# A two-layer graph network in fp32 on one core: late relus, two more pairs by seven products, and the adjacency loaded behind the first statistics

## The chip, the cores and the metric

One core of one Trainium2 chip runs the whole kernel. The metric is the device time in microseconds (us). Besides timed runs there is one profiled execution, from which every duration below is taken. The engines are named as in the profile: PE (TensorE, matmuls and transposes), DVE (VectorE), ACT (ScalarE), POOL (GpSimd) and SP (SyncE, which here only issues transfers). Each engine works through its own queue in order and waits for the others by semaphores. All data is fp32; a product of 128 x 128 by 128 x 512 takes two matmul instructions in the trace, 0.43 us apart.

## The reference

Two residual layers on x of 16 images, 1024 nodes and 256 features. What matters, shortened:

```
h = relu(layernorm(x))
c_adj = mean of h over features;  A_s = symmetrized 2*| |sigmoid(c_m - c_n) - 0.5| - 0.5 |
g = relu((h^T @ (adj * A_s)) * para)                 # queries
k, v = h @ kv_w
x = x + attention(q, k, v), 4 heads of 64
h = relu(layernorm(x))
A_hat = D^-1/2 (adj + I) D^-1/2                      # same for all images
z1 = (A_hat @ h) @ W1^T + b1                         # 512 wide
z2 = relu(batchnorm(z1)) @ W2^T + b2                 # statistics over all 16 images
out = x + batchnorm(z2)
```

The two batch norms need statistics over all images. So the kernel has three stages: everything up to z1 for every image, then z2 for every image, then the output.

## The kernel before

**Start.** SP issues x of image 0 in four pieces (`load_x(0, 2)`, L188), then at once the eight 512 KB blocks of the adjacency (L202) and kv_w (L205). POOL meanwhile issues six small column transfers (b1, g1 and so on, L81). DVE takes the layer norm's statistics of the first four blocks of x (`Norm.stats`, L250 and L252), POOL the power -0.5 (L257), and DVE the shift (L263, placed behind the statistics of the next two blocks); ACT then normalizes (L278). PE's first work is `turn_adj(0)` (L957), the transposes of adjacency block 0, then the transposes that spread the row sums (L312 and L323), and after some ACT and DVE work the first graph product `f_gps` (L398).

**One image.** In `graph(b + 1, between)` PE multiplies h by eight weighted adjacency blocks (L398), with steps of other work put between the blocks by hand: `between[c]` lists what is issued on the other engines before block c. Among them, for image b, is its second layer norm: statistics at 2 and 4, and the relus of blocks 0 to 3 and 4 to 7 at 6 and 7 (L278, writing `f_h_b`). Then come the queries (L415, L416), the values (L423, copied by L430) and the keys. For b of 2 and above the keys are made by seven products in place of eight (L463 to L487): products add up in one PSUM bank x, and after each ACT copies the bank's state out (L474, L478, L482, L487) before the next product is added. Then `linear1` (also seven products, L690) needs sums of parts of h (`f_hs`, L683 to L686), and `linear1_seven` makes z1 (L796) and stores it to DRAM (L831). Then `attention`.

**End of stage 1.** After the last attention two linear 1 are left. In the first of them, `third()` transposes W2 through a PSUM tile of pool `ps_s` (`turned`, L1027) and ACT copies it (L1176). For the very last image z1 is made in the plain form (`linear1_out`, L877), with its first batch norm invertible in two halves.

**Last passes.** z1 is read back (`fetch`, L163), normalized by ACT (`relu_on`, L152) and multiplied by W2. Image 0 goes in the plain form (L1221, `plain`, `plain_out` L1349 on DVE), then `SEVEN`, images 1 to 12, by seven products for a pair of tiles (`Pair`, L1283: m1 to m7, `keep` copies on ACT at L1294, `add` on DVE at L1297), then `rest`, the four tiles of images 13 and 14, in the plain form, then the two tiles of image 15, which stay in PSUM. A pair uses six slots of pool `io` (15 slots of 4 KB a partition) and, for block (1, 0), one of the four slots tagged `z`. PSUM in this stage is one pool of eight banks, which is closed before the last two tiles.

**Output.** After the second batch norm's statistics, z2 of each image is scaled (`finish`, L1498 on ACT or L1500 on DVE), transposed by PE (L1516), added to x1 (L1549, DVE) and sent out on ACT's queue (L1550). x1 of images 0 to 6 and 9 has been loaded ahead (`load_x1`, L1205), images 7 and 8 follow when the last tiles' `z` slots are free, and each further image when an output transfer frees its slots.

The stages are written under a manual schedule: the order in the source is the order on every engine, SP included.

## Time and profile before

| | us |
|---|---|
| median of 3 runs (lowest, highest) | 2447.41 (2447.23, 2450.25) |
| the profiled execution | 2446.91 |
| its span, first to last instruction | 2445.0 |
| PE busy | 2390.1 (98%) |
| DVE busy | 1777.3 (73%) |
| ACT busy | 1316.7 (54%) |
| POOL busy | 308.2 (13%) |
| granted TensorE clock, mean | 0.996 |
| first graph product begins | 17.48 |
| last passes begin (first z2 product) | 2169.44 |
| first output transfer is issued | 2382.70 |

Moved over the span: 169.35 MB read from DRAM and 71.10 MB written. A row of the time line gives the start, the length, the engine, the line, the operation with output and inputs, their shape and the count; a bracket at its end gives the idle time of that engine before it and what ended it. A row of stretches gives, for each engine, the busy time with the number of instructions, and then the clock, the share of time in which the 16 DMA engines were busy, and GB/s. In the chain of waits the columns are the start, the length and what the time was spent on. Under "who waited for it" stand the total time and the number of waits. For each transfer the trace also holds the times at which its 16 parts landed.

### The profile page before, as it was taken

What the parts mean: (1) busy time and instruction counts of PE and PEld (TensorE: products, weight loads), DVE (VectorE), ACT (ScalarE), POOL (GpSimd) and SP (SyncE); (2) the same over time, 40 slices, a digit from 0 to 9 for tenths busy, and PEclk for the clock granted to TensorE, in tenths of its full rate; (3) what the DMA queues carried; (4) which work ended last, traced back from release to release, by engine and by line L of the source; (5) the groups of instructions that cost most, each with busy time, mean ns of one, the idle gap of its engine ahead of it and who ended that gap; (6) DMA issues with size and microseconds to landing.
All of it is one profiled execution on the core that took longest, in us unless ns stands there. A gap on an engine that the chain in (4) does not pass through costs nothing.

```text
span 2445.0 us, 24677 instructions
## 1 busy us (share of the span) xinstructions
PE 2390.1 (98%) x8050; PEld 1052.2 (43%) x8050; DVE 1777.3 (73%) x2440; ACT 1316.7 (54%) x1918; POOL 308.2 (13%) x546
## 2 busy tenths in 40 slices
PE   8999999999999999999999999999999999999995
PEld 4443444434343434344443434343444434434444
DVE  6878677685959596776859595958777687747746
ACT  6845556454636464654546364645546465346633
POOL 2030202020110303020202002030202020000000
PEclk9999999999999999999999999999999999999998
DMA  5041414232322424141422233241414211455569
GB/s 185 9 139 61 151 61 142 69 109 68 109 86 75 128 64 148 61 151 61 125 78 90 79 100 103 67 144 61 151 61 138 74 49 51 142 194 172 167 214 377
DMA packets 176632, 275.76 MB, mean 113 GB/s; under 512 B 37872, under 2 KB 121328, under 8 KB 176496
## 3 DMA queue, kind: packets, MB, share of 16 engines
q1 hardware_dynamic: 156336, 241.55, 30.6%
q0 software_dynamic: 15552, 15.77, 2.5%
q10 hardware_dynamic: 4608, 16.78, 1.7%
q8 instruction: 66, 1.08, 0.2%
q14 instruction: 70, 0.57, 0.1%
HBM read 169.35 MB, written 71.10 MB: 98 GB/s over the span
## 4 chain that ended last, share of the span: by engine, by line
PE 79%; DVE 11%; SPq 3%; DMA 3%; ACT 2%; issue 2%; POOL 1%; DVEq 0%; ACTq 0%; POOLq 0%
PE f_aps L690 15%; PE f_s L501 14%; PE f_o L542 14%; PE f_gps L398 13%; PE f_zps L796 5%; DVE f_acc L518 3%; PE f_vps L423 3%; PE f_zx L1283 3%; SPq L606 3%; PE f_zm L1283 2%; PE f_kpsx L464 2%; PE f_z2ps L1221 2%; PE f_kps L464 1%; ACT f_h_b L278 1%; DVE f_w L349 1%
## 5 line engine op out<-in xcount | busy, mean ns | idle before, releaser
L509 ACT ACTIVATE f_p<-f_s 128x1024 f32<-128x1024 f32 x512 | 477.3, 1048 | 153.4 <-PE f_s L501 153.3
L518 DVE TENSOR_TENSOR f_acc<-f_acc,f_p 128x1024 f32<-128x1024 f32 x384 | 470.4, 1225 | 41.1 <-ACT f_p L509 0.5
L501 PE MATMUL f_s<-f_qT,f_kT 64*128 64x512 f32 x2048 | 456.8, 596 | 0.0
L542 PE MATMUL f_o<-f_p,f_v 128*64 128x512 f32 x2048 | 453.6, 595 | 0.0
L398 PE MATMUL f_gps<-f_w,f_h_a 128*128 128x512 f32 x1024 | 444.7, 594 | 0.3 <-DVE f_w L336 0.3
L368 POOL DMA_DIRECT2D f_hT<-f_hQ x480 | 235.8, 499 | 1219.9 <-PE f_gps L398 1170.7
L501 PEld LDWEIGHTS f_s<-f_qT,f_kT 64*128 64x128 f32 x2048 | 190.7, 185 | 263.6 <-ACT f_p L509 117.3
L398 PEld LDWEIGHTS f_gps<-f_w,f_h_a 128*128 128x128 f32 x1024 | 192.8, 190 | 247.0 <-issue 229.8
L542 PEld LDWEIGHTS f_o<-f_p,f_v 128*64 128x64 f32 x2048 | 141.4, 137 | 304.3 <-issue 253.9
L349 DVE SCALAR_TENSOR_TENSOR f_w<-f_w,f_adj 128x1024 f32<-128x1024 f32 x127 | 153.8, 1212 | 38.8 <-ACT f_w L348 38.8
L345 ACT ACTIVATE f_w<-f_row,f_col 128x1024 f32<-128x1024 f32 x127 | 147.0, 1158 | 28.1 <-DMA f_row<-frow 18.7
L278 ACT ACTIVATE f_h_b<-f_x,f_shift_b,f_rstd_b 128x256 f32<-128x256 f32 x128 | 64.7, 587 | 161.0 <-DVE f_shift_b L263 161.0
L348 ACT ACTIVATE f_w<-f_w 128x1024 f32<-128x1024 f32 x127 | 134.3, 1058 | 4.0
L690 PE MATMUL f_aps<-f_ahatT,f_hs 128*128 128x512 f32 x256 | 115.1, 592 | 0.0
L690 PE MATMUL f_aps<-f_t,f_hs 128*128 128x512 f32 x256 | 112.5, 592 | 1.3 <-DVE f_hs L684 1.3
L423 PE MATMUL f_vps<-f_kvw,f_hT 128*128 128x256 f32 x512 | 113.1, 379 | 0.0
L690 PE MATMUL f_aps<-f_ahatT,f_h_b 128*128 128x512 f32 x256 | 112.6, 592 | 0.0
L278 ACT ACTIVATE f_h_a<-f_x,f_shift_a,f_rstd_a 128x256 f32<-128x256 f32 x126 | 73.8, 587 | 63.4 <-DVE f_shift_a L263 63.4
L423 PEld LDWEIGHTS f_vps<-f_kvw,f_hT 128*128 128x128 f32 x512 | 97.3, 190 | 20.1 <-issue 7.4
L515 DVE TENSOR_TENSOR f_acc<-f_p,f_p 128x1024 f32<-128x1024 f32 x64 | 76.2, 1191 | 15.3 <-ACT f_p L509 15.3
L584 ACT COPY f_recs<-f_rec 32x32 f32<-32x32 f32 x128 | 31.5, 246 | 98.6 <-DVE f_rec L576 97.5
L569 ACT COPY f_parts<-f_red 32x64 f32<-32x64 f32 x128 | 39.1, 305 | 78.4 <-DVE f_red L534 77.3
(230 smaller groups left out, 2694.8 us busy)
## 6 DMA issues: line engine op xcount, KB each, us to landing
f_t<-ft SPq DMA_DIRECT2D x84, 512.0 KB, 6.9
fz<-f_z SPq DMA_DIRECT2D x64, 512.0 KB, 9.7
f_x<-in_x_dram SPq DMA_DIRECT2D x31, 1024.0 KB, 7.8
f_zb<-fz SPq DMA_DIRECT2D x36, 512.0 KB, 4.2
f_para<-in_L_gnn_para_dram SPq DMA_DIRECT2D x32, 512.0 KB, 4.4
f_att<-f_oT SPq DMA_DIRECT2D x512, 32.0 KB, 1.9
fx<-f_x SPq DMA_DIRECT2D x16, 1024.0 KB, 6.5
f_x1t<-fx SPq DMA_DIRECT2D x32, 512.0 KB, 6.6
```

What stands on the lines that cost most here:

```text
L278: nc.scalar.activation(self.h[:, c, :], self.xt[:, c, :], AF.Relu, bias=self.shift[:, c : c + 1], scale=self.rstd[:, c : c + 1], accum_out ...
L345: nc.scalar.activation(w, rows[b], AF.Abs, bias=cols[b][:, c : c + 1], scale=0.5 / C)
L348: nc.scalar.activation(w, w, AF.Tanh)
L349: nc.vector.scalar_tensor_tensor(w, w, 1.0, adj_t[c], ALU.subtract, ALU.mult)
L368: queue.dma_start(to[ts(k, 32), ts(a, 32 * NC)], t[ts(a, 32), k].rearrange("i c r -> i (c r)"),)
L398: nc.tensor.matmul(gps[d][:, ts(g, 512)], hs[b][:, c, ts(d, P)], w[:, ts(g, 512)], start=(c == 0), stop=(c == NC - 1),)
L423: nc.tensor.matmul(ps[:, i, :], hT[e][:, ts(c4 + i, P)], kvw_t[:, e, C : 2 * C], start=(e == 0), stop=(e == CC - 1),)
L501: nc.tensor.matmul(ps[:, e, :], kT[rows_e, pair, ts(m, P)], qT[rows_e, pair, ts(g, 512)], start=True, stop=True,)
L509: nc.scalar.activation(p, ps, AF.Exp)
L518: nc.vector.tensor_add(acc_of[s], acc_of[s], p)
L542: nc.tensor.matmul(o_of[s][e * HD : (e + 1) * HD, :], v[:, m, ts(2 * pair + e, HD)], p[:, e, :], start=(m == 0), stop=(m == NC - 1),)
L690: nc.tensor.matmul(ps, left[:, m, :], right(m), start=not more and m == 0, stop=(m == KH - 1), skip_group_check=more,)
```

## The change

It has these parts:

1. The adjacency's blocks and kv_w are issued by `load_adj()`, after the statistics of the first four blocks of x. To tie them together, these statistics are written to a tile in the slot of block 6 (tag `w2n`), so that block 6 is issued first and has to wait for their last reader; the other blocks follow in SP's order.
2. Of the second layer norm's relus, blocks 4 to 7 move out of `between[7]` to the list `"late"`: for b of 2 and above two run after the first key copy and two after the second, else before the keys.
3. The sums of h for the very last linear 1 are made in the one before it, by `ending()`, ahead of four statistics.
4. W2's transposes go through two PSUM tiles of the pools `ps_o` and `ps_t` in place of one of `ps_s`.
5. `SEVEN` goes to image 14, and `rest` is gone. What was loaded behind image 12 (tiles 30 and 31, x1 of images 0 to 6) is loaded in the turns of images 13 and 14. In the turn of image 14 ACT's relus of tiles 30 and 31 stand before `keep(0, 1)` and `keep(1, 1)`.
6. PSUM in the last passes is two pools of four banks: `ps_x` for the bank x and the last tiles, `ps_z` for the rest. Image 0's tiles take their banks in the order 1, 0. The pool `io` is opened before `big`, so its addresses change.
7. The first pair's loads are issued before image 0's products, block (1, 0) last, and `plain_out` copies on ACT.
8. In the output, c = 0 of images 0 to 3 is scaled before the second half's statistics are known, c = 1 of images 1 to 3 is scaled by ACT, and for image 0 this comes after the additions.

```diff
@@ start
-        adj_t = []
-        for c in range(NC):
...
+        adj_t = {}
         kvw_t = big.tile([P, CC, 2 * C], F32, tag="kvw", name="f_kvw")
-        nc.sync.dma_start(kvw_t, kv_w.rearrange("(c p) d -> p c d", p=P))
+        def load_adj():
+            for c in (LASTING.index("w2n"), *range(NC)):
+                if c in adj_t:
+                    continue
...
+                nc.sync.dma_start(t, adj[ts(c, P), :])
+                adj_t[c] = t
+            nc.sync.dma_start(kvw_t, kv_w.rearrange("(c p) d -> p c d", p=P))
...
+            own = norm.st
+            norm.st = lasting.tile([P, NC, 6], F32, tag="w2n", name="f_st_a0_first")
             norm.stats(0, HALF)
+            norm.st = own
+            load_adj()
             norm.invert(0, HALF)
@@ graph
+            late = between.get("late", ())
             if b < 2:
+                for step in late:
+                    step()
...
             nc.vector.tensor_add(c(0, 0), c(0, 0), m2)
+            late[0]()
             mult(x, sums[:, 1], t2, True)
             nc.scalar.copy(c(1, 0), x)
+            late[1]()
...
-                    7: [lambda: norm.relu(4, NC)],
+                    "late": [lambda: norm.relu(4, 6), lambda: norm.relu(6, NC)],
@@ linear 1
+        def sums_of_h(b, h1):
...
+            s1, s2, s3, s4 = made or sums_of_h(b, h1)
...
             store(0, 1)
+            ending()
             stats(1, 1)
             stats(0, 1)
...
-                        nc.scalar.copy(
-                            w2T.rearrange("p f c -> p (f c)"), turned(w2n, CC, FC, "w2")
-                        )
+                        for n, (pool, tag) in enumerate(((ps_o, "o"), (ps_t, "t"))):
+                            ps = pool.tile([P, 2, CC, P], F32, tag=tag, name=f"f_w2ps_{n}")
...
+                        lambda: made.extend(sums_of_h(b, norm.h)),
...
+                    linear1_all(b, norm.h, thirds, nothing, nothing, nothing, made=made)
@@ last passes
+        io = stage.enter_context(tc.tile_pool(name="fio", bufs=NH * (AHEAD - 3) + 1))
         big = stage.enter_context(tc.tile_pool(name="fbig2", bufs=1))
-        io = stage.enter_context(tc.tile_pool(name="fio", bufs=NH * (AHEAD - 3) + 1))
...
+            ps_x = stage.enter_context(tc.tile_pool(name="fps_x", bufs=4, space=PSUM))
             zps = ExitStack()
-            ps_z = zps.enter_context(tc.tile_pool(name="fps_z", bufs=8, space=PSUM))
+            ps_z = zps.enter_context(tc.tile_pool(name="fps_z", bufs=4, space=PSUM))
...
                     self.b[0, 0] = fetch(t0, 0, new("b11"))
-                    self.b[1, 0] = fetch(t0, 2)
                     self.b[0, 1] = fetch(t1, 0, new("b12"))
                     self.b[1, 1] = fetch(t1, 2, new("b22"))
+                    self.b[1, 0] = fetch(t0, 2)
...
-                    nc.vector.tensor_copy(place(t, c), ps[c])
+                    nc.scalar.copy(place(t, c), ps[c])
...
-            SEVEN = range(1, B - 3)
-            rest = range(2 * SEVEN[-1] + 2, TT - 2)
+            SEVEN = range(1, B - 1)
...
+            begun = {t: [bank(f"f_z2ps_{t}_{c}") for c in range(CC)] for t in (1, 0)}
+            first = pairs[SEVEN[0]]
+            first.load()
...
                     pairs[p + 2].load()
+                elif p + 1 in pairs:
+                    for t, f2 in ((TT - 2, 0), (TT - 2, 2), (TT - 1, 0)):
+                        zs[t, f2] = fetch(t, f2)
+                    load_x1(0)
+                else:
+                    zs[TT - 1, 2] = fetch(TT - 1, 2)
+                    for n in range(1, AHEAD - 3):
+                        load_x1(n)
...
+                else:
+                    relu_all(TT - 2)
                 now.m6()
                 now.keep(0, 1)
                 now.m7()
...
+                else:
+                    relu_all(TT - 1)
                 now.m5()
                 now.keep(1, 1)
@@ output
+            EARLY = 4
+
             def by_scalar(b, c):
-                return c == 0 or b % 2 == 1
+                return c == 0 or b % 2 == 1 or 0 < b < EARLY
...
-                    finish(0, 0)
-                    finish(1, 0)
+                    for n in range(EARLY):
+                        finish(n, 0)
...
+                if b > 0:
+                    finish_soon(True)
                 for h in range(NH):
                     nc.vector.tensor_add(xt[h], xt[h], outs[h])
                     nc.scalar.dma_start(out_v[:, 4 * h : 4 * h + 4, :], xt[h])
+                if b == 0:
+                    finish_soon(True)
+                finish_soon(False)
```

## The prediction

> **What bounds it now.** The shares come first: TensorE (PE) is busy 98% of the span at a clock of 0.996, so work on another engine counts only where PE stands still for it, or where PE has nothing left to do. I then looked for those places with the time line of PE, in order of time, reading the bracket that names the idle time and what ended it. They lie at the two ends.

> The start, in the chain of waits: PE's first work waits for the first adjacency block, and all that follows hangs on it without a gap.

> ```profile
> 2.78 7.35 DMA f_adj<-in_adj_dram
> 10.13 0.14 issue
> 10.27 1.94 PE f_adjps L957 x8
> 12.21 1.71 PE f_rps L312 x8
> 13.92 1.57 PE f_rps L323 x8
> ```

> The middle repeats every 133.3 us per image with PE closed up, but for one wait, which the question "who waited for L474" gives: the copy of the first key product comes late, and in 4 of 14 images PE itself stops.

> ```profile
>   PEld f_kpsx L464: 13.2, 14
>   DVE f_kT L476: 8.5, 4
>   PE f_kpsx L464: 2.9, 4
> ```

> The end of linear 1 and the last passes, PE's time line: seven stops in 240 us.

> ```profile
> 2123.34 1.98 PE L796 MATMUL f_zps<-f_zt,f_w1T 128*128 128x512 f32 x4 [1.39 <-ACT f_w2T L1176]
> ...
> 2136.90 7.11 PE L690 MATMUL f_aps<-f_t,f_hs 128*128 128x512 f32 x16 [1.28 <-DVE f_hs L684]
> ...
> 2169.44 14.00 PE L1221 MATMUL f_z2ps<-f_z,f_w2T 128*128 128x512 f32 x32 [1.40 <-ACT f_z L886]
> ...
> 2186.60 1.98 PE L1283 MATMUL f_zm<-f_z,f_w2T 128*128 128x512 f32 x4 [1.44 <-ACT f_z L152]
> 2189.77 1.96 PE L1283 MATMUL f_zx<-f_zt,f_w2s 128*128 128x512 f32 x4 [1.18 <-DVE f_zt L1278]
> ...
> 2200.57 1.98 PE L1283 MATMUL f_zm<-f_zt,f_w2T 128*128 128x512 f32 x4 [1.98 <-DVE f_z L1297]
> ...
> 2331.32 3.70 PE L1221 MATMUL f_z2ps<-f_zz,f_w2T 128*128 128x512 f32 x8 [1.39 <-ACT f_zz L152]
> ...
> 2363.31 10.54 PE L1221 MATMUL f_z2ps<-f_z,f_w2T 128*128 128x512 f32 x24 [0.83 <-issue]
> ```

> The output, by stretches (the last two numbers are the DMA share and GB/s): from 2390 us on all DMA engines are full, and the end is the end of the transfers. PE work saved before 2380 us still moves the end, because DMA is only 46% busy from 2340 to 2375 us.

> ```profile
> 2375.00:2380.00 5.00, 3.45 (x19) 2.55 (x17) 2.10 (x10) 0.88 (x1) 0.55 (x1) 1.00 0.60 198
> 2380.00:2385.00 5.00, 3.28 (x24) 2.57 (x24) 4.21 (x6) 3.86 (x4) 0.00 (x0) 1.00 0.65 254
> ...
> 2395.00:2400.00 5.00, 3.64 (x28) 2.74 (x26) 4.83 (x5) 1.98 (x2) 0.00 (x0) 1.00 1.03 415
> ```

> A stop is counted below from start to start of the matmuls less their usual pitch (0.43 us for one of 512 columns), so it is about 0.15 us more than the bracket.

> **Adjacency behind the first statistics: +0.9 us.** SP's nine issues (eight blocks, kv_w) now wait for the fourth bn_aggr, which ends at 5.32 us; before, the first was issued at 2.78. Behind them on SP stand the second image's x and W1, but x waits for the last relu at 12.1 us anyway. What could this buy? The third and fourth pieces of x land at 7.14 and 8.28 us, and DVE and ACT wait for them. [...] In the trace six of the 16 parts of the third piece land by 5.17 us, the other ten each right after a part of b1's small GpSimd transfer; the first adjacency packet moves only at 5.4 us, and the blocks then land in order, 10.13, 11.46, 12.75 us, 1.3 apart. [...] so the adjacency, behind x in SP's queue, doesn't hold x up, and waiting frees nothing. [...] the slowest DMA engine is busy with x until nearly 8 us in both kernels, so the first block to go lands near 10.1 as before. But that is now block 6, and block 0, which PE needs, comes second: 11.4, a loss of 1.3. [...] were the adjacency what holds x, x would be whole at 6, the shift could run when GpSimd's power is done (7.3, now 8.2), and block 0 could land at 9.6: a gain of 0.7. At the worst both transfers start a latency late: a loss of 1.8. I take 0.9, nearer to the row. W1 is needed by PE at 25.4 and lands at 24.9; it shifts no more than PE does.

> **Late relus: −3.4 us.** Of the eight relus (8 in 4.04 us) four move behind the first two key copies. ACT then reaches the queries 2.0 us earlier, and the stops, 0.92, 1.07, 1.09 and 0.40 us in four images (3.48 together), all shorter than 2.0, go. The price is to be hidden between the copies of L474, L478 and L482, where ACT idles 1.22 us each time; two relus take 1.01 and a tail of 0.08. It fits by 0.1 us. Without that cover each overrun would stop PE, as the next product accumulates in the bank being copied. In the image seen the last relu would end near 295.8, and the sums of linear 1 want h at 297.7. Bounds: 3.5 gained, 0.5 lost (0.02 per copy). For b = 1 only transfers are passed: nothing.

> **W2's transposes and the sums of h: −1.9.** The stops are 1.55 (m4 waits for the bank of the transposes) and 1.44 (the second factor s2 waits behind four bn_stats, 2.46 us). Both causes go, 2.99 together. But next is DVE: m4 is released by L852 at 2127.8, behind relu work that hangs on the attention's last addition, not on PE. PE now wants the bank at 2127.0 and gets it 0.8 later; s2 is ready at 2134.3, just before its product at about 2135, which was at 2136.9. I take 1.9; bounds 1.4 and 2.9.

> **First products of the last passes: −1.3.** Stop 1.57, for a bank still read by ACT (L886). Two other banks, long free, are taken now; next is ACT's relu of the first half, which ends at 2168.1, 0.25 after PE is free. Bounds 0 and 1.6.

> **The first pair: −3.4.** Its three stops are 1.61, 1.34 and 2.14, 5.09 together. Its loads were issued at 2172.2 to 2174.0, each behind the z slot that PE freed at 2172.9; now three of four go out right after the last store (2169.7), and block (1,0) after the slot. They land some 2.4 us earlier, and the fourth near 2181.7, its relu ending at 2183.3. Then ACT, not the load, is late: four plain_out copies (0.5 each) have moved to it, standing behind that relu, and m2 needs the bank that the third frees: about 2185.0, where PE would be there at 2183.4. So 1.6 of the 5.1 is given back. DVE, free of the copies, no longer causes the stop at m4. Bounds 1.5 and 5.1.

> **Two more pairs by seven products: −3.4.** The plain tiles of images 13 and 14 are 64 matmuls in the trace (8 + 56 of L1221 on f_zz); a pair by seven products is 28, in 12.02 us. 64 − 56 = 8, by 0.429 us: 3.4, all on PE. The additions (six of 0.67 to 1.23 us a pair) lie beside PE as in the twelve pairs before.

> **The seams: −1.2.** The stops before the plain tiles (1.55) and before the last tiles (0.99) go. A new one comes in pair 14: no next product stands between m5 and m3, so m3 waits for keep(1, 1), and that stands on ACT behind the relu of tile 31, whose second half is loaded only after m2 frees its slot: about 1.3. Bounds 0.5 and 2.3.

> **Output: −0.7.** Two c = 0 blocks more are scaled by ACT in its idle 4.26 us before 2380.1 (2 × 1.19), and DVE loses one scaling of 0.81 (image 2) before the DMA engines are full. The transfers past that point are the same bytes. Bounds 0 and 1.2. Reordered pools move addresses; I see no wait that they add.

> **The sum:** +0.9 − 3.4 − 1.9 − 1.3 − 3.4 − 3.4 − 1.2 − 0.7 = −14.4. The profiled execution took 2446.9 (span 2445.0), so 2432.5; the median of the runs shown is 0.5 higher, 2447.4, so 2433.0.

> **Rivals.**
> *Given back at both ends* (0.17): block 0 lands late (+1.8, 0.9 more), the first pair gains only its 1.5 (1.9 less), the seams 0.5 (0.7 less), the output nothing (0.7 less): −10.2, 2437.2. For it: all are queues worked out only to within a microsecond. Against: each needs its bad end.
> *x is freed* (0.12): the start gains 0.7 and the first pair all its 5.1: −17.7, 2429.7. For it: the wait for x's last pieces is real (DVE stands 4.1 us for x); against: the parts that landed late follow b1, not the adjacency.
> *The transfers are late for the output* (0.06): x1 of images 1 to 6, 6.3 MB, now starts in pair 14, with 3.1 MB more before the output. At 417 GB/s that is 22.6 us in some 33; if three images were still under way when the output starts, 7.5 us come back: 2440.5. Against: 10 us of slack.
> *Slower* (0.04): the relus behind the key copies don't fit. The two relus hold the accumulating product in each of 14 images twice; from an overrun of 0.51 us each (14.4 / 28) the change loses. If they ran with nothing overlapped, at the mean of 0.587 and a wait of about 0.6 before each pair, 1.8 us in a window of 1.22: 28 × 0.6 = 16.8 lost, 2449.8. Against: 8 in 4.04 us.
> The forecast keeps 0.61.

> **Numbers.** The terms' bounds, taken as independent, make about ±3; the range 2429.0 to 2438.5 takes in the second rival and most of the first. 0.2% (4.9 us) is what a measurement can tell from none. Faster 0.95, within it 0.02, slower 0.03.

> **What would show it.** Block 0's landing and the first f_gps (17.48 before): later means right. No idle before f_kpsx in any image. One short stop near 2127, none at the h sums. 14 pairs at 12.0 us. m2 of the first pair waiting for ACT. DMA full from about 2375 to the end. The forecast is wrong if f_gps starts earlier, if the key section takes over 6.4 us in all images, or if the DMA engines stop being full in the output.

## The result, and the profile after

| | before | after |
|---|---|---|
| median of the runs of both in one session (lowest, highest) | 2447.3 (2442.22, 2450.25) | 2435.02 (2433.29, 2436.68) |
| the profiled execution, its span | 2446.91, 2445.0 | 2434.83, 2432.8 |
| first f_gps begins | 17.48 | 18.99 |
| first z2 product begins | 2169.44 | 2165.46 |
| PE's first transposes of the output | 2377.93 | 2363.99 |
| first output transfer issued | 2382.70 | 2368.75 |
| from there to the last landing, to the end of the span | 60.2, 62.3 | 61.6, 64.1 |

The ratio is 0.9953 with a 95% interval of 0.9941 to 0.9966: some 12 us faster, where 14.4 less was forecast (2433.0, with 2435.02 inside the range). The table says where to look: the start lost 1.5, everything up to the output gained 15.5 beyond that, and the output gave back 1.8. The same places as before follow, in order of time.

The chain of waits at the start (start, length, what). Block 0 now lands at 11.93, and PE, ACT and the first product hang on it as before.

```profile
5.75 6.18 DMA f_adj<-in_adj_dram
11.93 0.14 issue
12.06 1.94 PE f_adjps L977 x8
14.00 1.72 PE f_rps L316 x8
...
15.74 0.69 ACT f_w L333
```

Who waited for the copy of the first key product (L481, which was L474): only the weight loads, 0.7 an image, and PE itself no longer stands among them.

```profile
who waited for it (us, times):
  PEld f_kpsx L471: 9.8, 14
```

PE's time line at the end of linear 1, in the last passes, and in pair 14. Of the eight stops shown of before one is left, 1.41 before the first z2 product, and two are new: 0.83 for the bank of m4 and 1.31 in pair 14. The first pair (2179.30 on) has none.

```profile
2126.05 7.11 PE L707 MATMUL f_aps<-f_ahatT,f_h_b 128*128 128x512 f32 x16 [0.83 <-DVE f_z L869]
...
2165.46 14.00 PE L1265 MATMUL f_z2ps<-f_z,f_w2T 128*128 128x512 f32 x32 [1.41 <-ACT f_z L904]
2179.30 1.88 PE L1327 MATMUL f_zx<-f_zb,f_w2T 128*128 128x512 f32 x4
2181.01 1.88 PE L1327 MATMUL f_zm<-f_z,f_w2T 128*128 128x512 f32 x4
...
2345.91 1.98 PE L1327 MATMUL f_zx<-f_zb,f_w2s 128*128 128x512 f32 x4 [1.31 <-ACT f_z L1338]
```

The output by stretches of 3.41 us (after the length: PE, PEld, DVE, ACT, POOL busy with counts, then the granted clock, the DMA share and GB/s). PE is busy 1.34 of 3.41 us in the second stretch, and in the third, where the output's transposes begin in earnest, its clock is 0.50.

```profile
2361.36:2364.78 3.42, 2.90 (x18) 2.36 (x16) 1.06 (x4) 2.85 (x3) 0.00 (x0) 1.00 0.92 352
2364.78:2368.19 3.41, 1.34 (x11) 0.86 (x9) 2.13 (x8) 1.95 (x2) 0.56 (x1) 1.00 0.76 279
2368.19:2371.60 3.41, 2.83 (x13) 2.83 (x14) 2.48 (x3) 1.33 (x2) 0.00 (x0) 0.50 0.61 243
```

PE's own rows show the two stops in those stretches, 1.77 and 0.88. They are the same in the kernel before (first two rows: before, last two: after); in the changed kernel the second stretch holds the first stop whole and 0.30 of the second.

```profile
2380.75 1.09 PE L1516 MATMUL f_outps<-f_ident,f_z 128*128 128x128 f32 x8 [1.77 <-DVE f_z L1500]
2382.72 2.23 PE L1516 MATMUL f_outps<-f_ident,f_z 128*128 128x128 f32 x16 [0.88 <-DVE f_x1t L1549]
...
2366.80 1.09 PE L1544 MATMUL f_outps<-f_ident,f_z 128*128 128x128 f32 x8 [1.77 <-DVE f_z L1526]
2368.77 4.38 PE L1544 MATMUL f_outps<-f_ident,f_z 128*128 128x128 f32 x24 [0.88 <-DVE f_x1t L1583]
```

That leaves four questions: why the start lost more than forecast, why the stop before the first z2 product stayed, why the first pair gained 5.1 and not 3.4, and what took 1.8 in the output. The runs below answer them, and test the late relus. Each was timed beside the kernel before; the differences from the changed kernel are mostly under 2 us, within the intervals of those ratios, so they are read in the profiles, by the stretch that the edit touches.

### The profile page after: what moved, and what is told of

Same layout as the page of the kernel before. It is cut to its first block, busy times and chain, and to the rows that moved or that the text cites. A ratio compares the mean times of both kernels' runs of the same rounds, so it can differ in the third digit from the quotient of the medians.

```text
span 2432.8 us, 24669 instructions
## 1 busy us (share of the span) xinstructions
PE 2386.7 (98%) x8042; PEld 1053.3 (43%) x8042; DVE 1782.0 (73%) x2441; ACT 1325.9 (55%) x1932; POOL 308.1 (13%) x546
## 4 chain that ended last, share of the span: by engine, by line
PE 96%; DMA 1%; DVE 1%; ACT 1%; issue 0%; POOL 0%; ACTq 0%; DVEq 0%; SPq 0%; POOLq 0%
PE f_s L510 19%; PE f_o L551 18%; PE f_gps L402 18%; PE f_aps L707 16%; PE f_zps L813 6%; PE f_vps L427 5%; PE f_zx L1327 4%; PE f_zm L1327 3%; PE f_kpsx L471 2%; PE f_kps L471 1%; PE f_z2ps L1265 1%; PE f_zps L895 1%; PE f_kps L444 1%; DMA out_dram<-f_x1t 1%; DVE f_x1t L1583 1%; PE f_zps3b L813 0%
```

## The experiments

### The start: what the wait costs

The first run issues the blocks in the order 0 to 7, at once behind x:

```diff
-            for c in (LASTING.index("w2n"), *range(NC)):
+            for c in range(NC):
...
+        load_adj()
...
-            norm.st = lasting.tile([P, NC, 6], F32, tag="w2n", name="f_st_a0_first")
             norm.stats(0, HALF)
-            norm.st = own
-            load_adj()
```

> The changed kernel (profiled span 2432.8), but SP issues the adjacency at once behind x, in the order 0 to 7, as before. Theory 1 (block 0 stands second and lands late: 11.93 against 10.13): the first f_gps goes back from 18.99 to about 17.5, the third and fourth pieces of x land again near 7.1 and 8.3, and the span falls by 1.5, to about 2431.3. Rival (the deferral buys something further on, since x is read sooner): the first f_gps comes no earlier than 18.6 and the span doesn't fall.

The second keeps the wait and lays the first statistics in the slot of block 0:

```diff
-    LASTING = ["z"] * 4 + [None] * 2 + ["w2n", "w2T"]
+    LASTING = ["w2n"] + ["z"] * 4 + [None] * 2 + ["w2T"]
```

> The changed kernel, but the tile of the first statistics lies in the slot of block 0 in place of block 6, so that block 0 is the first to go behind them. Theory 1 (the wait itself costs nothing; only block 0's second place does): block 0 lands about where block 6 did, near 9.6 to 10.7, x's last pieces stay at 6.3 and 7.15, PE transposes the row sums as soon as ACT and DVE have them (about 11.3, was 13.8), the first f_gps is at 16.5 to 17.2 (18.99), and the span falls by 1.8 to 2.5, to about 2430.7: below the kernel that issues at once (2431.3). Rival (waiting for the statistics costs by itself): the first f_gps is at 17.8 or later and the span stays above 2431.5.

e1: PE begins on block 0 at 10.10, f_gps begins at 17.39, the span is 2431.7 (time 2433.22, ratio 0.9951, 0.9934 to 0.9967). e2: f_gps at 15.79, 3.2 earlier than in the changed kernel, but the first z2 product at 2163.94, no earlier than in e1 (2163.86): 1.7 of the 3.2 is lost again, 1.3 of it in one stop 10 us later. Span 2431.0, time 2432.07 (0.9946, 0.993 to 0.9963). PE's time line of e2 shows where:

```profile
9.66 1.94 PE L977 MATMUL f_adjps<-f_ident,f_adj 128*128 128x128 f32 x8 [9.66 <-DMA f_adj<-in_adj_dram]
...
15.79 3.67 PE L402 MATMUL f_gps<-f_w,f_h_a 128*128 128x512 f32 x8 [0.26 <-DVE f_w L340]
...
25.88 1.06 PE L1047 MATMUL f_w1ps<-f_ident,f_w1n 128*128 128x128 f32 x8 [1.15 <-DMA f_w1n<-in_L_gnn_W_dram]
```

W1, behind 1 MB of x in SP's queue, lands at 25.75 and is the next bound. So the third run, otherwise like the second, moved it:

```diff
+            w1n = w4.tile([P, FC, C], F32, tag="w4", name="f_w1n")
+            nc.sync.dma_start(w1n, W1.rearrange("(f p) d -> p f d", p=P))
             xs[1] = load_x(1)
```

> Block 0 first behind the statistics, and W1 is issued ahead of the second image's x. With block 0 first alone the first f_gps was at 15.79, but PE then stopped 1.32 for W1, which lands at 25.75 behind 1 MB of x. Theory 1b (that transfer is what takes the gain back): W1 lands near 22.5, the stop goes, the stretch from the first f_gps to the first z2 product falls from 2148.1 to 2146.5 to 2146.9, and with f_gps at 15.8 the first z2 product is at 2162.3 to 2162.8 (2165.46 in the changed kernel). Rival (PE is held by what stands behind: the weighting of the blocks on ACT and DVE, or the second image's x landing late): the stretch stays at 2147.8 or more.

W1 lands at 22.06, its stop is gone, and the stretch from f_gps to the first z2 product is 2146.60, as in the changed kernel (2146.47). Here f_gps began at 16.98, so the first z2 product came at 2163.58 and not at the 2162.3 to 2162.8 expected; span 2431.4, time 2431.89 (0.9939, 0.9923 to 0.9956).

The scatter of this start has to be known before a single f_gps is believed. PE's first transposes of block 0 began at 10.27, 10.10 and 9.20 in three executions that issue at once (the third is e9, below), at 11.12 to 12.50, mean 11.9, in eight with block 0 second, and at 9.66, 9.73 and 10.51 in three with block 0 first. The first f_gps: 15.92 to 17.48, mean 16.9; 18.37 to 19.86, mean 19.0; 15.79 to 17.83, mean 16.9. So theory 1 is half right. Second place costs 2.1 us on average; for the wait as such no cost shows, within the scatter of three executions each. Nor does a gain: that e2 would go below issuing at once isn't borne out. x's last two pieces land at 6.2 to 6.7 and 7.0 to 7.4 in all eleven executions in which the adjacency waits. Where it doesn't, they land at 7.1 to 7.6 and 8.2 to 8.3 in two of three, and at 6.3 and 7.35 in the third (e9). So x was held up in two executions; the mean f_gps is the same either way.

### The first z2 product: the pool, not the bank

```diff
-            ps_z = zps.enter_context(tc.tile_pool(name="fps_z", bufs=4, space=PSUM))
+            ps_z = zps.enter_context(tc.tile_pool(name="fps_z", bufs=2, space=PSUM))
+            ps_y = zps.enter_context(tc.tile_pool(name="fps_y", bufs=2, space=PSUM))
-                return (pool or ps_z).tile([P, 512], F32, tag="z", name=name)
+                    pool = (ps_y, ps_y, ps_z, ps_z)[len(turns) % 4]
...
-            begun = {t: [bank(f"f_z2ps_{t}_{c}") for c in range(CC)] for t in (1, 0)}
+            begun = {t: [bank(f"f_z2ps_{t}_{c}") for c in range(CC)] for t in (0, 1)}
```

> The changed kernel, but the pool of four banks for the last passes is split in two pools of two, and tile 0 of image 0 takes the one that lies where ps_o and ps_t lay. Theory 2 (the first product waits because its bank belongs to a pool that lies over ps_s, and such a pool is handed over only when the last reader of ps_s is done, L904 at 2165.41, whatever the bank): the stop of 1.57 before the first f_z2ps shrinks to 0.2 or less, nothing new comes before 2200, and the span falls by 1.2 to 1.5, to about 2431.4. Rival (the wait is for the relu of the data, or the first pair's ACT queue takes the time back): the stop stays at 1.5 or the gain is found again as a stop between 2175 and 2190, and the span stays at 2432.8.

PE's time line of this run: the product starts behind the last one of linear 1, and nothing follows.

```profile
2159.75 4.03 PE L895 MATMUL f_zps<-f_aggT,f_w1T 128*128 128x512 f32 x9
2163.61 13.90 PE L1270 MATMUL f_z2ps<-f_z,f_w2T 128*128 128x512 f32 x32
2177.34 1.88 PE L1332 MATMUL f_zx<-f_zb,f_w2T 128*128 128x512 f32 x4
```

From f_gps to the first z2 product it is 2144.89, 1.58 less than 2146.47, and the first pair is as dense as in the changed kernel. Span 2429.1, time 2431.96 (0.9948, 0.9932 to 0.9965); the span lies 3.7 below that of the changed kernel, more than the stop, and the rest is in the output (below). In the changed kernel the bank of the first product (tile 0, c = 0) still lies over ps_s. ACT's rows of that kernel give the last two readers of ps_s:

```profile
2160.66 1.26 ACT L904 ACTIVATE f_z<-f_zps,f_b 128x512 f32<-128x512 f32 x2 [2.17 <-PE f_zps L895]
...
2164.14 1.27 ACT L904 ACTIVATE f_z<-f_zps,f_b 128x512 f32<-128x512 f32 x2
```

The bank's own last reader is the first of them, done at 2161.92, before PE was free. But PE waited for the other one, the last reader of all of ps_s, at 2165.41 (the bracket of 1.41 before 2165.46). In e3 the bank in a pool that lies only over ps_o and ps_t didn't wait (2163.61, without a bracket).

### The output: half the clock

Two runs: one has the scaling in the old order, the other fills PE's wait for the second half's statistics.

```diff
-            EARLY = 4
+            EARLY = 2
...
-                return c == 0 or b % 2 == 1 or 0 < b < EARLY
+                return c == 0 or b % 2 == 1
...
-                if b > 0:
-                    finish_soon(True)
+                finish_soon(True)
```

```diff
+                    for n in range(12):
+                        nc.tensor.transpose(outs[1][:, n % 4, ts(1, P)], ident, ident)
                     ready[0, 1] = z2[:, 1, 0, :]
```

> The changed kernel, but the output's scaling in the old order (two images ahead of the statistics, odd images' c = 1 on ACT, ACT's scaling ahead of the additions). From the first output transfer to the end of the span the kernel before takes 62.3, the changed one 64.05. Theory 3 (the new order of scaling costs it): back to about 62.3, span about 2431. Rival a (a half-speed window of the clock fell on the first transposes of the output, 2368.2 to 2371.6, and the transfers got into another order; chance of the windows): the time from first output to end depends on where such a window falls and not on the edit: 64 with one, 62.5 without one in the first 4 us. Rival b (x1 loads and addresses): stays at 64 without such a window.

> The changed kernel, with 12 transposes of the identity into the unused half of an output bank, later overwritten, in PE's 1.8 us wait for the second half's statistics (1.4 us of work, none of it on the path). In the runs so far a window of 3.41 us in which PE was busy 0.38 to 0.39 (2364 to 2368) was followed by one at half clock, and the time from the first output transfer to the end was then 63.1 to 64.6; after 0.48 or 0.51 it was not, and the end came after 62.3 to 62.5. Theory 5 (the half clock is the output's lost time): the windows before the output are busy 0.6 or more, the clock stays full until 2380, and first output to end is 62.2 to 62.8: span about 2431.2. Rival (the order of the scaling or of the transfers costs it): 63.7 or more with the clock at full speed.

e4: 63.1 from first output to end, with a half-clock window from 2370.6 (first output at 2371.11); span 2434.2, time 2434.05 (0.9953, 0.9937 to 0.997). A second window of that kind hit it at 2346.7, right behind the stop in pair 14, and its 3.41 us cost PE about 1.7. e7, in the same kind of stretches as above:

```profile
2363.08:2366.49 3.41, 2.88 (x18) 2.35 (x17) 1.05 (x4) 2.85 (x3) 0.00 (x0) 1.00 0.89 333
2366.49:2369.90 3.41, 2.66 (x23) 2.19 (x21) 2.13 (x8) 1.95 (x2) 0.56 (x1) 1.00 0.82 264
2369.90:2373.32 3.42, 2.60 (x20) 2.13 (x21) 3.37 (x4) 1.33 (x2) 0.00 (x0) 1.00 0.68 268
```

PE is busy 2.66 in place of 1.34 in the stretch of the wait, and the clock stays at 1.00. First output to end is 63.2, between the two expectations; span 2433.7, time 2433.45 (0.9946, 0.993 to 0.9963). What decides is the time from the first output transfer to the last landing, since 2.1 to 3.3 us more follow the last landing and vary without a pattern that I see:

| first output to last landing | us |
|---|---|
| before, twice (clock full) | 60.2, 59.9 |
| new order, clock full (e3, e5, e10) | 59.8, 59.6, 59.9 |
| new order, wait filled (e7, e11) | 59.9, 60.1 |
| new order, half clock (changed kernel, e1, e2, e6, e8, e12) | 61.6, 61.7, 61.1, 61.3, 61.3, 61.3 |
| old order, half clock (e4) | 61.0 |

With the clock full at the first transposes it is 60.2 at most, with half clock there 61.0 at least, whatever the order. (Later in the output every profile has half-clock windows: in before from 2404.52 and 2411.35, in the changed kernel from 2388.67, 2398.91 and 2405.74.) In the new order half clock costs 1.5. At full clock the new order gains 0.2 (its third output goes out 2.4 behind the first, not 3.0), which is hardly more than the scatter; at half clock the one profile of the old order is 0.4 below the mean of the new. So theory 3 has no room for 1.8, and neither has rival b. PE's stops are the same in both kernels, so where the window falls is chance: in the two profiles of before the window with the longer stop was busy 0.51 and 0.56, and half clock did not follow.

### The late relus

```diff
-                    "late": [lambda: norm.relu(4, 6), lambda: norm.relu(6, NC)],
+                    7: [lambda: norm.relu(4, NC)],
...
-            late[0]()
-            late[1]()
```

> The changed kernel, but blocks 4 to 7 of the second layer norm's relus go back to between[7]. Theory 4 (the prediction's: ACT reaches the queries 2.0 later, and that alone made PE stop ahead of the first key product of the next half): stops before f_kpsx return in about four of 14 images, 3.4 to 3.6 together, and the time from the first f_gps to the first z2 product grows from 2146.5 to about 2150.0. Rival (the stops went for another reason, such as the start's new phase): no stop of over 0.3 returns there and the stretch stays at 2146.5 to 2147.

One stop came back, 1.32 in one image, and the stretch grew by 1.47, to 2147.94 (span 2432.5, time 2434.86, ratio 0.9956, 0.9939 to 0.9972). Neither text had that. GpSimd's time line of this run shows the image that stopped, against the one before it:

```profile
949.99 1.66 POOL L261 TENSOR_TENSOR f_rstd_b<-f_var_b,f_mhalf 128x8 f32<-128x8 f32 x1 [3.49 <-DVE f_var_b L260]
...
1082.68 0.50 POOL L372 DMA_DIRECT2D f_hT<-f_hQ  x1 [0.22 <-issue]
1084.24 0.50 POOL L372 DMA_DIRECT2D f_hT<-f_hQ  x1 [1.06 <-DMA f_hT<-f_hQ]
1084.75 1.67 POOL L261 TENSOR_TENSOR f_rstd_b<-f_var_b,f_mhalf 128x8 f32<-128x8 f32 x1
```

In image 8 the power -0.5 stood behind two transfers that POOL issues, one of which waited for a landing: it began 1.8 after its input. DVE's shift and all of ACT's chain (relus, queries, values, the key copy) moved with it, and PE stopped:

```profile
1094.93 1.13 PE L471 MATMUL f_kpsx<-f_kt,f_kt 128*128 128x512 f32 x2 [1.16 <-ACT f_kT L481]
```

So the 2.0 us by which ACT is earlier are slack for delays that differ from execution to execution. A second profile of the kernel before (e9, below) shows how much they differ.

The late power is not the only such delay. In the first profile of before it accounts for one stop of four (the same image, 1.6 late); in the other three, and in both of e9, POOL was on time, but DVE's addition of the attention (L614) waited long for a transfer. DVE's rows of the kernel before, in an image with a stop and in one without:

```profile
946.73 1.23 DVE L614 TENSOR_TENSOR f_x<-f_x,f_att 128x1024 f32<-128x1024 f32 x1 [4.66 <-DMA f_att<-f_oT]
...
1213.25 1.23 DVE L614 TENSOR_TENSOR f_x<-f_x,f_att 128x1024 f32<-128x1024 f32 x1 [2.70 <-DMA f_att<-f_oT]
```

In the two profiles of before, the five images that stopped without a late power have the addition 22.9 to 23.8 behind the start of the graph product that it runs beside, those without a stop at 22.8 or less. In the changed kernel one image has it at 23.2, and PE doesn't stop: that is the slack at work. Why these transfers land late isn't shown.

### The first pair: chance or program, copies or order

Three edits, besides the second profile of before (e9). The loads stand behind image 0's products again (e8):

```diff
-            first.load()
             for t in range(2):
                 plain(t, begun[t], 0)
...
+            first.load()
             for k, j in ((0, 0), (0, 1), (1, 1), (1, 0)):
```

plain_out copies on DVE (e10):

```diff
-                    nc.scalar.copy(place(t, c), ps[c])
+                    nc.vector.tensor_copy(place(t, c), ps[c])
```

Block (1, 0) is loaded second (e12):

```diff
+                    self.b[1, 0] = fetch(t0, 2)
                     self.b[0, 1] = fetch(t1, 0, new("b12"))
                     self.b[1, 1] = fetch(t1, 2, new("b22"))
-                    self.b[1, 0] = fetch(t0, 2)
```

> The changed kernel, but the first pair's loads are issued behind image 0's products again (block (1, 0) still last, plain_out still on ACT). Theory 6 (the three stops of the first pair were waits for the loads, and going out 3 to 4 us earlier took all three): stops of 2.5 to 4 in all come back between the first f_zx and 2200, most of them before m2 and m4. Rival (the copies on ACT in place of DVE were what took them): less than 1.0 comes back.

> The kernel before, profiled a second time. Theory 7 (two of the terms are drawn anew in each execution: the stops ahead of the key products, since GpSimd's power -0.5 comes late in some images, and the first pair's loads, whose 4 KB packets took 0.2 to 0.47 on average and up to 1.6 in the first profile of before, 0.16 to 0.2 in that of after): the stops before f_kpsx sum to another amount than 3.48, and the three stops of the first pair to another amount than 5.09, each by over 0.7. Rival (both are fixed by the program): 3.3 to 3.7 in the same four images, and 4.8 to 5.4 in the first pair.

> The changed kernel, but plain_out copies on DVE again. Theory 8 (DVE's queue caused the last stop of the first pair, 2.14 before m4, and moving the copies to ACT removed it): a stop of 1.5 to 2.2 comes back before m4 (about 2191). Rival (that stop was late only because the loads were): DVE begins the first pair's sums about 2178 in place of 2186 after 8.3 more of the stretch, its copies then fit, and less than 0.5 comes back.

> The changed kernel, but block (1, 0) of each pair is loaded second again and not last. The copies on DVE alone brought back 1.48 before m2 and none of the other two stops (1.35 and 2.15 in the kernel before). Theory 9 (those two are the load order: blocks (0, 1) and (1, 1) stand behind (1, 0), which waits for its slot, and DVE's sums with them): the first sums begin 3 to 4.5 later than the 12.2 after the first z2 product seen now, and stops of 2.5 to 3.7 in all come back between the first f_zx and 2200. Rival (they come only if copies and order are both as before, since DVE then has both): less than 1.0 comes back.

e8: no stop at all in the first pair; its loads went out 2.6 us after the first z2 product, as in the changed kernel. SP gets to them no earlier, with or without the products behind them: after the last z1 store it stands 2.2 us for DVE's last aggregation of the first batch norm, which ends 2.5 behind the first z2 product. From SP's waits around it, the same line in the changed kernel and in e8:

```profile
SPq L163 <- DVE f_bn_mv L112: 2.2, 1, 2.2
```

Theory 6 falls (span 2433.8, time 2434.39, 0.995, 0.9933 to 0.9967). e9 splits: the key stops sum to 0.67 in two images (first profile: 3.48 in four), so they are drawn anew in each execution; the first pair's are 4.9, the same three, so they belong to the program. PE's time line of e9:

```profile
2182.96 1.98 PE L1283 MATMUL f_zm<-f_z,f_w2T 128*128 128x512 f32 x4 [1.25 <-ACT f_z L152]
2186.13 1.96 PE L1283 MATMUL f_zx<-f_zt,f_w2s 128*128 128x512 f32 x4 [1.19 <-DVE f_zt L1278]
...
2196.94 3.12 PE L1283 MATMUL f_zm<-f_zt,f_w2T 128*128 128x512 f32 x4 [1.99 <-DVE f_z L1297]
```

The last row takes 3.12 for four matmuls, where 1.98 is usual: the stops left a window busy only 0.42, and half clock followed, 1.7 lost on top (span 2442.8, time 2444.68 in its one run). e10 brings back one stop, 1.48, but before m2 and not m4, which neither of its texts had (span 2433.0, time 2435.17, one run):

```profile
2180.11 1.88 PE L1327 MATMUL f_zx<-f_zb,f_w2T 128*128 128x512 f32 x4
2183.31 1.95 PE L1327 MATMUL f_zm<-f_z,f_w2T 128*128 128x512 f32 x4 [1.32 <-ACT f_z L1338]
```

ACT's copy named there had ended at 2182.61; what ended last is DVE's first plain_out copy (2182.52 and 0.68), which frees the bank that m2 takes. e12 brings back 2.51, as theory 9 has it in sum, but all of it before m2, and with it a half-clock window that costs 1.7 more (span 2436.5, time 2438.37, one run):

```profile
2183.05 2.66 PE L1327 MATMUL f_zm<-f_z,f_w2T 128*128 128x512 f32 x4 [2.35 <-ACT f_z L1393]
2185.51 2.94 PE L1327 MATMUL f_zx<-f_zt,f_w2s 128*128 128x512 f32 x4
```

DVE's sums begin 16.2 after the first z2 product (changed kernel: 12.2; before: 16.4). So the order of the loads makes the sums and ACT's relus 4 us earlier, and the copies on ACT take DVE's part of the queue away; it took both to remove all the stops. Why the order matters so much is in the DMA's stretches. The kernel before, 5 to 9 us behind its first z2 product (last two numbers: DMA share, GB/s):

```profile
2174.44:2176.44 2.00, 2.00 (x6) 0.80 (x6) 0.52 (x2) 2.00 (x4) 0.00 (x0) 1.00 0.76 223
2176.44:2178.44 2.00, 2.00 (x6) 0.92 (x5) 0.00 (x0) 1.42 (x3) 0.00 (x0) 1.00 0.72 123
```

The changed kernel in the same place:

```profile
2170.46:2172.46 2.00, 2.00 (x6) 0.80 (x6) 0.52 (x2) 2.00 (x4) 0.00 (x0) 1.00 0.95 334
2172.46:2174.46 2.00, 2.00 (x6) 0.92 (x5) 0.00 (x0) 2.00 (x4) 0.00 (x0) 1.00 0.97 328
```

Blocks (0, 1) and (1, 1) landed 13.4 and 14.7 after the first z2 product in before, 7.9 and 10.6 in the changed kernel, while (1, 0), second or last, landed at 12.0 and 11.9. With (1, 0) second it was the same in e9 (252, then 160 GB/s) and in e12 (240, then 158). So it goes with the order. SP issues the other two 1.1 us later behind (1, 0)'s slot; why the transfers also run at half the rate isn't settled.

### All of it together

The kernel of e6 with e3's banks, e7's filled wait, and in pair 14 the last half tile's relu behind `keep(1, 1)`:

```diff
-                    relu_all(TT - 1)
+                    relu_on(zs[TT - 1, 0], 0)
                 now.m5()
                 now.keep(1, 1)
+                if not soon:
+                    relu_on(zs[TT - 1, 2], 2)
```

> The changed kernel with block 0 first, W1 ahead of x, own banks for the first product, the last half tile's relu behind keep(1, 1) (the 1.47 stop of pair 14), and the filled wait. By the separate measurements: the first f_gps at 16 to 17 in place of 18.99 (2.0 to 3.0), no stop before the first f_z2ps (1.6), none in pair 14 (1.5), no half clock at the output (1.4 less than the changed kernel's profile): span 2425.3 to 2426.5, and about 7 below the changed kernel in time, 2427 to 2429. If the gains hide behind one another (DMA in the output, or ACT's queue in the first pair), the span stays above 2428.

2429.22 (2428.65 to 2430.61, 5 runs), ratio to before 0.9935 (0.9922 to 0.9949), span 2428.6. The changed kernel's 2435.02 was timed beside other runs of before: by the ratios the gain over it is 0.0018, about 4.4 us, and the intervals overlap. The stop before the first z2 product and the half clock at the output are gone, but f_gps drew 17.83, and in pair 14 a stop of 0.84 stays:

```profile
2339.91 1.88 PE L1332 MATMUL f_zx<-f_zb,f_w2s 128*128 128x512 f32 x4
2342.47 1.98 PE L1332 MATMUL f_zx<-f_zb,f_w2s 128*128 128x512 f32 x4 [0.68 <-ACT f_z L1343]
```

m3 adds to the bank that keep(1, 1) copies, and with no other product in between the copy of 0.58 lies open. The expected 2425.3 to 2426.5 took the start at its best, this stop at nothing, and the end behind the last landing at 2.1 to 2.5 (here 3.2). The span lies above the 2428 that was set as the sign of gains hiding behind one another; these three misses, 0.8 to 1.8, 0.84 and 0.7 to 1.1, account for it without that.

## Why the prediction was right, point by point

The range was kept and most of the mechanisms were as told; three terms (first products, first pair, output) failed in whole or in part, and their errors partly cancelled. (The text counts seven stops in PE's 240 us where its own block shows eight; the terms use all eight.)

- **Adjacency, +0.9: too small.** The mechanism is as forecast: block 6 lands first, at 9.51, and block 0 comes second, at 11.93. The first block to land isn't later for the wait (before: 10.13). The term was sized by "11.4, a loss of 1.3"; in eight executions the loss at f_gps is 2.1, beyond the bound of 1.8 on average, 1.5 in the profiled pair. "Waiting frees nothing" failed: x's last pieces, at 6.2 to 6.7 and 7.0 to 7.4, came about 1 us sooner than in two of three executions at once (7.1 to 7.6 and 8.2 to 8.3). That the adjacency, behind x in SP's queue, doesn't hold x up was the author's estimate, and those two contradict it.
- **Late relus, −3.4: right between the two profiles (3.48), but not a property of the program.** "The stops, 3.48 together, all shorter than 2.0, go": they did, in every image of all eleven profiles with the late relus. Undone, they came back as 1.3, and a second profile of before had 0.67. The worth is 0.7 to 3.5 an execution. The forecast was sized on the profile with 3.48 and is compared here with that same profile, so the match says little of the size. The price was nothing, as forecast: two relus fit between the copies.
- **W2's transposes and sums, −1.9: measured −2.0.** Both stops went, and the one forecast to come ("gets it 0.8 later") is there at 2126.05, behind DVE's L869: 0.83 in the bracket, 0.99 by the prediction's count. Read in the profile alone; neither was undone by itself.
- **First products, −1.3: failed, 0.** The step "two other banks, long free, are taken now" was wrong: the bank's own history didn't count, since its pool lay over one still in use. With a pool of its own the gain was 1.58.
- **First pair, −3.4: measured −5.1, the mechanism half wrong.** The failed step is "the fourth near 2181.7": block (1, 0) landed at 2177.33, since its slot was free as soon as SP came to it. So ACT's copies, which were to give 1.6 back, weren't late. e12 shows the forecast wait exactly, m2 behind ACT's L1393, where that block's neighbours are late. The step "three of four go out right after the last store (2169.7)" was wrong too: they go out 2.6 behind the first z2 product in either place (e8). What made the sums early is the order among the loads, which the term did not count.
- **Two more pairs, −3.4.** Not tried alone; in the trace pairs begin every 12.02 us to the last, as forecast (once 0.34 more, for a small check product).
- **Seams, −1.2: measured −1.1.** 1.55 and 0.99 went, and the stop in pair 14 came, 1.47 where 1.3 was forecast, behind the relu named.
- **Output, −0.7: measured +1.8.** The term left out the clock. 1.5 of it is a half-clock window on the first transposes (2368.19 to 2371.60, clock 0.50), about 0.4 the end behind the last landing; the edit itself gained 0.2 at full clock. The DMA engines were full to the end, as forecast, but from 2380, not 2375 (share 0.92 from 2375 to 2380, 1.03 in the next 5 us, 1.02 from 2420 to 2425).

The terms as measured, 1.5 − 3.5 − 2.0 − 5.1 − 3.4 − 1.1 + 1.8, make −11.8 of the −12.2 between the profiles. So the forecast of −14.4 was right by its sum partly by luck: errors of +0.6, +1.3 and +2.5 stood against one of −1.7, and two of the terms, the key stops and the half clock, are drawn anew in each execution. The rival in which both ends give back (2437.2) had the loss at the start and the missing gain of the output right in place; the first pair and the seams did not give back as it said.

## What to carry to other kernels

Reordering loads behind a wait is judged by which transfer goes first, not by the wait (here second place cost block 0's consumer 2.1 us on average, and the wait showed no cost): look at the block that the first consumer needs. A new PSUM pool over an old one waited here for the old one's last reader (a stop of 1.41, and 1.58 gained without it), so the first tile of a new stage should lie in a pool over banks that nobody reads any more. And a stop of PE can cost more than its length: where stops left PE busy 0.38 to 0.42 of a window of 3.41 us here, half clock followed and took 1.5 to 1.7 on top. A second profile of the same kernel tells which terms of a sum are the program's and which were drawn.

## What the runs showed of the hardware

**GpSimd's queue.** A power of 1.66 us began 1.8 after its input because a transfer issued ahead of it on GpSimd waited 1.06 for a landing; DVE and ACT came late with it, and PE stopped 1.16 (the bracket).

**Equal loads at unequal rates.** The same 512 KB blocks, 5 to 9 us behind the first z2 product, were read at 223 and 123 GB/s in one order, 334 and 328 in the other; two more executions with the slow order had 240 to 252 and 158 to 160. The cause is open.
